# The drain of a fused attention and layer-norm kernel, reordered

## The chip, the cores and the metric

The kernel runs on one core of a Trainium2 chip. The metric is device time in microseconds (us), median of several executions. The profile is one execution of the same program, seen by the hardware profiler; its times count from the first instruction. Engines: PE multiplies matrices (PEld loads its weights), DVE, ACT and POOL work on vectors, SP issues transfers.

## The reference

Inputs: x (4096 x 512), adj (4096 x 4096, about 0.4% of it entries up to 1e9, the diagonal among them), W (512 x 4 heads x 512), a (4 x 1024). All are 32-bit floats.

```
ht  = (x @ W) per head                            # 4 x 4096 x 512
e   = leaky_relu(src[i] + dst[j], 0.01) + adj     # src, dst: ht times the halves of a
att = softmax(e) over j
out = layernorm(x + mean over heads of att @ ht)
```

Where one entry of a row of adj leads all others by far, the softmax is one there and zero elsewhere, in every head. Then row i is layernorm(x[i] + x[j] @ mean of W over heads), with j the column of the row's largest entry. The kernel computes that for all rows, tests with a bound on src and dst whether every row's lead suffices, and has a general path for the case that one doesn't. With these inputs the general path isn't entered.

## The kernel before

There are 32 row blocks of 128 rows. For each block the kernel loads 2 MB of adj (line 127; blocks 28 to 30 in two pieces, block 31 in four), DVE takes maxima of short segments of each row (203), the best segment (210) and its place (212). POOL fetches that segment of the row again by an indirect transfer (223, tile lead); DVE finds the column in it (264) and the second largest value (258, find_inner). For block 31 the column is searched in the whole row at once (272). POOL gathers the x rows of the columns (244, 249; tile y). PE transposes them (278), ACT copies the result (280; tile yt), PE multiplies with the mean of W (297). x itself is added on PE by a matmul with the identity (290, residual).

The schedule is written out by hand: each engine runs its instructions in the order in which the program emits them, across all engines. Loop step t takes adj of block t, the column of block t - 2, the product of block t - 3, the statistics of block t - 4 on ACT (356 to 364) and, a few steps later, the normalisation on ACT (finish, 382). For the statistics' square root comes first root (367), then a reciprocal on DVE and two small instructions on POOL (rstd). Transfers go out on SP in order; a buffer of adj is reused after six blocks, so load t + 5 is issued in step t.

Behind the loop comes the drain. Blocks 24 to 27 (BEHIND to LATE - 1) were put by without x (347), and x is added behind their late load (351, POOL for 24 to 26 and DVE for 27). ACT makes the statistics of 24 to 26 and POOL their factors with a power (375 to 377); for 27 to 31 DVE does it with BN instructions (moments, 402 to 408; factor, 411; normalise, 418). Block 31 is multiplied in two halves (391). The bound of the test needs the square norm of every row of x (row_norm, 341; a maximum over all, 489 to 499); the test (505 to 511) sets a flag for each row, PE counts them (515), DVE makes of that the number of bad rows of each block and in all (519 to 522). Stores go out on SP: 0 to 23 as they become ready, then 28 and 29, 24 and 25, 26 and 27, 30, 31 (666 to 668).

In `tile("px", bufs=1)` one PSUM buffer serves the steps of the bound and the count in turn.

Of the kernel before, what the change touches and what calls it, by code (L numbers as in the profile page):

```python
# [21 lines left out]
P = 128  # L22
C = 512
# [9 lines left out]
@with_exitstack  # L33
def gat_resnorm_kernel(
    ctx: ExitStack,
    tc: tile.TileContext,
    x: bass.AP,
    adj: bass.AP,
    W: bass.AP,
    a: bass.AP,  # L40
    out: bass.AP,
):

    nc = tc.nc
# [12 lines left out]
    leading_rows(tc, x, adj, W, a, out, ident, n_bad, any_bad)  # L65

    flag = nc.values_load(any_bad[0:1, 0:1], min_val=0, max_val=N)
    with tc.If(flag > 0, preferred_fallthrough_block=True, label="general"):
        general(tc, x, adj, W, a, out, ident, n_bad)


@with_exitstack
def leading_rows(ctx, tc, x, adj, W, a, out, ident, n_bad, any_bad):

# [16 lines left out]
    BEHIND = LATE - Q  # L91

    landing = ctx.enter_context(tc.tile_pool(name="landing", bufs=1))
    landing.tile([P, 56], F32, name="pad")
    hold = landing.tile([P, NB, D], F32, name="hold")
    a_rows = landing.tile([2 * H, D], F32, name="a_rows")
    adj_pool = ctx.enter_context(tc.tile_pool(name="adj_pool", bufs=AHEAD + 1))
# [88 lines left out]
    nm = once.tile([P, NB], F32, name="nm")  # L186
    sd = once.tile([P, NB], F32, name="sd")
    lead_by = once.tile([P, 1], F32, name="lead_by")

    def span_of(ib):  # L190
        return next(k for k, (_, lo, hi) in enumerate(spans) if lo <= ib < hi)
# [68 lines left out]
    def find_column(ib):  # L260
        if ib < BEHIND:
            find_inner(ib)
        within = small.tile([P, 8], U32, name="within")
        nc.vector.max_index(within, top[:, ib, :], lead_of[ib])  # L264
# [18 lines left out]
    def turn(ib):  # L283
        yt_of[ib] = turned_rows(y_t.pop(ib))
# [54 lines left out]
    def row_norm(ib):  # L339
        sq = rows.tile([P, D], F32, name="sq")  # L340
        nc.scalar.activation(sq, hold[:, ib, :], AF.Square, accum_out=xx[:, ib : ib + 1])  # L341
# [7 lines left out]
    def add_x(engine, ib):  # L349
        o = o_ps[ib] = o_ps["by"][:, ib - BEHIND, :]  # L350
        engine.tensor_add(o, o, hold[:, ib, :])

    def stats(ib):
        o, i = o_ps[ib], slice(ib, ib + 1)
# [11 lines left out]
    def root(i):  # L366
        nc.scalar.activation(sd[:, i], sd[:, i], AF.Sqrt, bias=eps, scale=1.0 / D)

    def rstd(i):
        nc.vector.reciprocal(sd[:, i], sd[:, i])  # L370
# [114 lines left out]
    def bound(part):  # L485

        if part == 0:
            xm = once.tile([P, 1], F32, name="xm")
            nc.vector.tensor_reduce(xm, xx, axis=AX.X, op=OP.max)
            px = of_bound[0] = psum.tile([1, P], F32, name="px", bufs=1)  # L490
            nc.tensor.transpose(px, xm, ident)
        elif part == 1:
            nc.vector.tensor_reduce(xg, of_bound[0], axis=AX.X, op=OP.max)
        elif part == 2:
            pb = of_bound[2] = psum.tile([P, 1], F32, name="px", bufs=1)
            nc.tensor.matmul(pb, ones[0:1, :], xg, start=True, stop=True)
        else:
            nc.vector.tensor_mul(lead_by, of_bound[2], vn)
            nc.vector.tensor_scalar(lead_by, lead_by, 1.05, 110.0, op0=OP.mult, op1=OP.add)

    gap = once.tile([P, NB], F32, name="gap")

    def test():
        a1 = top[:, :, 0]
        nc.vector.tensor_tensor(gap, top[:, :, 1], inner[:, :, 1], op=OP.max)
        size = once.tile([P, NB], F32, name="size")
        nc.vector.scalar_tensor_tensor(size, a1, -1.0, a1, op0=OP.mult, op1=OP.max)
        nc.vector.tensor_sub(gap, a1, gap)
        nc.vector.tensor_scalar(size, size, -(2.0 ** -22), lead_by, op0=OP.mult, op1=OP.subtract)
        nc.vector.scalar_tensor_tensor(gap, gap, 0.9999, size, op0=OP.mult, op1=OP.add)  # L510
        nc.vector.tensor_scalar(gap, gap, 0.0, None, op0=OP.is_gt)

    def count():
        pg = psum.tile([1, NB], F32, name="px", bufs=1)
        nc.tensor.matmul(pg, ones[:, 0:1], gap, start=True, stop=True)
        return pg

    def report(pg):
        nc.vector.tensor_scalar(n_bad, pg, -1.0, float(P), op0=OP.mult, op1=OP.add)
        total = once.tile([1, 1], F32, name="total")  # L520
        nc.vector.tensor_reduce(total, pg, axis=AX.X, op=OP.add)
        nc.vector.tensor_scalar(any_bad, total, -1.0, float(N), op0=OP.mult, op1=OP.add)

    x_at = {lo - 1 - lo // (5 * Q): (lo, Q) for lo in range(Q, BEHIND, Q)}
    squares = list(range(KB * H))
    squares_at = {t: 2 if t < 7 else 1 for t in range(3, 15)}
    COLUMN, PROJECT, STATS, BEHIND_ROOT = 2, 3, 4, 3
    FACTORS = (*((lo, lo + Q) for lo in range(0, BEHIND - Q, Q)), (BEHIND - 4, BEHIND - 2), (BEHIND - 2, BEHIND))
    FINISHED = {t: (t - 11,) for t in range(11, 28)}
    FINISHED |= {28: (17, 18), 29: (19, 20), 30: (21,), 31: (22,)}  # L530
    WHOLE = range(12, 20)
    END = (*range(1, 3), *range(5, 20))

    for t in range(NB):
# [2 lines left out]
        if t in x_at:  # L537
            load_x(*x_at[t])
        if t + AHEAD == NB - 1:
            load_x(LATE, Q)  # L540
        load_adj(t + AHEAD)
        middle = PIECES if t in END else 1 if t == NB - 1 else 2
        segment_maxima(t, 0, middle)
        if t >= COLUMN and t not in END and t != COLUMN + 1:
            find_column(t - COLUMN)
        if t not in END:
# [7 lines left out]
        if t + 1 in TABLED:  # L554
            clear_rows(t + 1)
        for lo, hi in FACTORS:
            if t == hi - 1 + STATS + BEHIND_ROOT:
                rstd(slice(lo, hi))
        if t < 2:
            mean_of_heads(t)  # L560
        elif t == 2:
# [97 lines left out]
    stats_of_half(NB - 1, 0)  # L659
    factor(NB - 2)  # L660
    normalise(NB - 2, o_ps.pop(NB - 2))
# [7 lines left out]


@with_exitstack
def general(ctx, tc, x, adj, W, a, out, ident, n_bad):

# [173 lines left out]
```

## Time and profile before

| | |
|---|---|
| median of 3 runs (lowest to highest) | 234.12 us (234.05 to 234.87) |
| the profiled execution | 234.12 us, its span 232.6 us |
| PE, DVE, ACT, POOL busy | 193.3, 191.2, 145.2, 105.6 us |
| moved by DMA | 96.32 MB, mean 414 GB/s |
| read from HBM, written to it | 88.54 MB, 8.39 MB |
| last store issued | 228.44 us |

The span runs from the first instruction to the last; the other 1.5 us lie around it. In the profile a line of a group names its source line, engine, operation, out<-in tiles and count, then busy time, mean ns of one, and the idle time of the engine before it with what ended it. A line of a timeline gives start, length, engine, line and tiles; idle time stands in brackets.

### The profile page before, as it was taken

What the parts mean: (1) busy time and instruction counts of PE and PEld (TensorE: products, weight loads), DVE (VectorE), ACT (ScalarE), POOL (GpSimd) and SP (SyncE); (2) the same over time, 40 slices, a digit from 0 to 9 for tenths busy, and PEclk for the clock granted to TensorE, in tenths of its full rate; (3) what the DMA queues carried; (4) which work ended last, traced back from release to release, by engine and by line L of the source; (5) the groups of instructions that cost most, each with busy time, mean ns of one, the idle gap of its engine ahead of it and who ended that gap; (6) DMA issues with size and microseconds to landing.
All of it is one profiled execution on the core that took longest, in us unless ns stands there. A gap on an engine that the chain in (4) does not pass through costs nothing.

```text
span 232.6 us, 2428 instructions
## 1 busy us (share of the span) xinstructions
PE 193.3 (83%) x581; PEld 92.5 (40%) x588; DVE 191.2 (82%) x300; ACT 145.2 (62%) x356; POOL 105.6 (45%) x239
## 2 busy tenths in 40 slices
PE   0068988788099998998999789979999989899990
PEld 0023443343044443443444344445444444445460
DVE  0448289899969997999799959987999999888881
ACT  3004113588076986797998578647777775399661
POOL 4020514515554556355635665644444545548300
PEclk9999999999769999999999999999999999999999
DMA  6999999999999999999999999999999999999985
GB/s 226 430 428 435 424 434 420 438 427 409 440 426 427 418 435 432 437 412 425 443 420 424 426 435 423 418 433 427 428 430 417 425 423 417 420 420 419 426 366 201
DMA packets 12834, 96.32 MB, mean 414 GB/s; under 512 B 2093, under 2 KB 2541, under 8 KB 7056
## 3 DMA queue, kind: packets, MB, share of 16 engines
q1 hardware_dynamic: 9216, 88.08, 89.7%
q0 software_dynamic: 3584, 8.03, 8.8%
q8 instruction: 5, 0.08, 0.1%
q14 instruction: 13, 0.11, 0.1%
q10 hardware_dynamic: 16, 0.02, 0.0%
HBM read 88.54 MB, written 8.39 MB: 417 GB/s over the span
## 4 chain that ended last, share of the span: by engine, by line
DMA 57%; DVE 23%; PE 9%; ACT 4%; issue 3%; POOL 2%; DVEq 0%; POOLq 0%; ACTq 0%
DMA adj_t<-in_adj_dram 54%; DVE seg L203 19%; PE o L297 5%; DMA y<-in_x_dram,col 3%; ACT sq L341 2%; PE o L391 2%; DVE at L212 1%; DVE top L210 1%; PE tp L278 1%; DMA a_rows<-in_L_gnn_a_dram 1%; PE o L290 1%; POOL lead L223 1%; ACT hold L382 1%; DVE within L264 1%; ACT adj_t L347 1%
## 5 line engine op out<-in xcount | busy, mean ns | idle before, releaser
L203 DVE TENSOR_REDUCE seg<-adj_t 128x128 f32<-128x2048 f32 (+5 forms) x58 | 143.8, 2496 | 30.2 <-DMA adj_t<-in_adj_dram 30.1
L297 PE MATMUL o<-w_sum,yt 128*128 128x512 f32 x248 | 113.2, 596 | 2.0 <-ACT yt L280 1.8
L297 PEld LDWEIGHTS o<-w_sum,yt 128*128 128x128 f32 x248 | 45.9, 191 | 52.6 <-issue 41.8
L223 POOL DMA_INDIRECT lead<-in_adj_dram,row x32 | 32.7, 1022 | 14.7 <-POOL row L219 14.7
L219 POOL TENSOR_TENSOR row<-at,first 128x1 uint32<-128x1 uint32 x32 | 6.0, 189 | 65.0 <-DVE at L212 46.3
L280 ACT COPY yt<-tp 128x512 f32<-128x512 f32 x33 | 19.1, 580 | 25.6 <-PE tp L278 25.4
L278 PE MATMUL tp<-ident,y 128*128 128x128 f32 x128 | 22.5, 299 | 12.9 <-DMA y<-in_x_dram,col 12.9
L278 PEld LDWEIGHTS tp<-ident,y 128*128 128x128 f32 x128 | 18.8, 208 | 26.7 <-issue 19.6
L290 PE MATMUL o<-hold,ident 128*128 128x512 f32 x52 | 27.4, 613 | 0.6 <-issue 0.6
L442 PE MATMUL o<-hold,ident 128*128 128x512 f32 x32 | 15.6, 645 | 14.8 <-DMA hold<-in_L_gnn_W_dram 14.8
L249 POOL DMA_INDIRECT y<-in_x_dram,col x20 | 21.6, 1082 | 7.8 <-POOL col L266 5.2
L341 ACT ACTIVATE sq<-hold 128x512 f32<-128x512 f32 x32 | 19.9, 624 | 0.0
L382 ACT ACTIVATE hold<-hold,nm,sd 128x512 f32<-128x512 f32 x24 | 19.0, 803 | 0.0
L327 ACT ACTIVATE off<-px,minus 128x128 f32<-128x128 f32 x20 | 7.3, 367 | 17.7 <-PE px L325 17.6
L364 ACT ACTIVATE sq<-hold,nm 128x512 f32<-128x512 f32 x24 | 17.3, 722 | 0.8
L443 ACT ACTIVATE w_sum<-o 128x512 f32<-128x512 f32 x4 | 2.4, 597 | 22.6 <-PE o L442 22.6
L337 PE MATMUL o<-z,pick 128*128 128x512 bf16 x54 | 15.4, 389 | 0.6 <-ACT off L327 0.4
L442 PEld LDWEIGHTS o<-hold,ident 128*128 128x128 f32 x32 | 6.5, 208 | 23.2 <-issue 21.2
L362 ACT ACTIVATE hold<-o 128x512 f32<-128x512 f32 x24 | 14.3, 597 | 0.8
L244 POOL DMA_INDIRECT y<-in_x_dram,col x12 | 11.9, 996 | 5.5 <-POOL col L266 5.2
L210 DVE MAX8 top<-seg 128x8 f32<-128x256 f32 (+2 forms) x32 | 11.6, 362 | 1.1
L239 ACT COPY y<-zero 128x512 f32<-128x512 f32 x20 | 12.1, 603 | 0.0
(116 smaller groups left out, 177.3 us busy)
## 6 DMA issues: line engine op xcount, KB each, us to landing
adj_t<-in_adj_dram SPq DMA_DIRECT2D x28, 2048.0 KB
hold<-in_x_dram SPq DMA_DIRECT2D x6, 1024.0 KB
adj_t<-in_adj_dram SPq DMA_DIRECT2D x6, 1024.0 KB
hold<-in_L_gnn_W_dram SPq DMA_DIRECT2D x2, 2048.0 KB
out_dram<-hold SPq DMA_DIRECT2D x7, 512.0 KB
out_dram<-hold SPq DMA_DIRECT2D x3, 1024.0 KB
adj_t<-in_adj_dram SPq DMA_DIRECT2D x4, 512.0 KB
hold<-in_x_dram SPq DMA_DIRECT2D x2, 512.0 KB
```

The source lines that it names most:

```text
L203: nc.vector.tensor_reduce(seg_of[ib][:, ts(k, N // e // n)], adj_t[ib][:, ts(k, N // n)].rearrange("p (s e) -> p s e", e=e), axis=AX.X, op ...
L223: nc.gpsimd.indirect_dma_start(out=lead, out_offset=None, in_=adj_segs[e], in_offset=bass.IndirectOffsetOnAxis(ap=row[:, :1], axis=0),)
L249: nc.gpsimd.indirect_dma_start(out=y_t[ib], out_offset=None, in_=x, in_offset=bass.IndirectOffsetOnAxis(ap=col[:, :1], axis=0), bounds_che ...
L278: nc.tensor.transpose(tp[:, kb, :], y[:, ds(kb, P, KB)], ident)
L280: nc.scalar.copy(yt, tp)
L290: nc.tensor.matmul(o_ps[ib], ident, hold[:, ib, :], start=start, stop=False)
L297: nc.tensor.matmul(o_ps[ib], yt_of[ib][:, kb, :], w_sum[:, kb, :], start=(start and kb == 0), stop=(kb == KB - 1),)
L337: nc.tensor.matmul(o_ps[ib], pick, z[k], start=(start and k == 0), stop=False)
L341: nc.scalar.activation(sq, hold[:, ib, :], AF.Square, accum_out=xx[:, ib : ib + 1])
L364: nc.scalar.activation(sq, hold[:, ib, :], AF.Square, bias=nm[:, i], scale=-float(D), accum_out=sd[:, i])
L382: nc.scalar.activation(hold[:, ib, :], o, AF.Identity, bias=nm[:, i], scale=sd[:, i])
L442: nc.tensor.matmul(o, ident, hold[:, w_at + kb * H + h, :], start=(h == 0), stop=(h == H - 1))
```

## The change

The drain and the steps that lead into it are reordered, and some of their work is done in another way:

- x of 28 to 31 was one load ahead of adj of 31. Now x of 28 and 29 stays there, and x of 30 and 31 goes behind adj of 31, between that of 24 and 25 and that of 26 and 27.
- Block 28 gets its x by DVE, PSUM plus x into PSUM, instead of a matmul; 29's residual matmul moves one step later.
- The factors of blocks 20 to 23 are made one step earlier, those of 22 and 23 on POOL a step behind their reciprocal. finish of 21 and 22 moves ahead in step 30, that of 23 into step 31.
- Row norms of 28 and 29 stay in step 31; 30 and 31 join the late ones.
- On POOL the adds of x to 24 and 25 go behind the gather of 30, the gather of 31's rows goes ahead of the fetch of its segment, and the adds to 26 and 27 follow; DVE adds no x to 27 any more.
- The factors of 24 and 25 and those of 26 are made apart.
- The test has five instructions instead of six, its last one also sums the flags of a row (accum_out), and it stands behind the normalisation of 29. The bound is one ACT instruction. The count is a 128x1 matmul ahead of the halves of 31, and the report one instruction; the counts for each block are made in the general path.

```diff
+    leads = keep.tile([P, NB], F32, name="leads")
...
-    landing.tile([P, 56], F32, name="pad")
+    landing.tile([P, 24], F32, name="pad")
...
+    def add_sums(ib, out):
+        nc.vector.tensor_add(out, o_ps[ib], hold[:, ib, :])
+        o_ps[ib] = out
...
-            nc.vector.tensor_mul(lead_by, of_bound[2], vn)
-            nc.vector.tensor_scalar(lead_by, lead_by, 1.05, 110.0, op0=OP.mult, op1=OP.add)
+            nc.scalar.activation(lead_by, of_bound[2], AF.Identity, bias=floor, scale=vn)
...
-        nc.vector.tensor_scalar(size, size, -(2.0 ** -22), lead_by, op0=OP.mult, op1=OP.subtract)
-        nc.vector.scalar_tensor_tensor(gap, gap, 0.9999, size, op0=OP.mult, op1=OP.add)
-        nc.vector.tensor_scalar(gap, gap, 0.0, None, op0=OP.is_gt)
+        nc.vector.scalar_tensor_tensor(
+            size, size, 2.0 ** -22, lead_by.to_broadcast([P, NB]), op0=OP.mult, op1=OP.add
+        )
+        nc.vector.scalar_tensor_tensor(
+            leads, leads, 0.9999, size, op0=OP.mult, op1=OP.is_gt, accum_out=leading
+        )
...
     def report(pg):
-        nc.vector.tensor_scalar(n_bad, pg, -1.0, float(P), op0=OP.mult, op1=OP.add)
-        total = once.tile([1, 1], F32, name="total")
-        nc.vector.tensor_reduce(total, pg, axis=AX.X, op=OP.add)
-        nc.vector.tensor_scalar(any_bad, total, -1.0, float(N), op0=OP.mult, op1=OP.add)
+        nc.vector.tensor_scalar(any_bad, pg, -1.0, float(N), op0=OP.mult, op1=OP.add)
...
-            load_x(LATE, Q)
+            load_x(LATE, 2)
...
-            for ib in (BEHIND, BEHIND + 2):
+            for ib in (BEHIND, LATE + 2, BEHIND + 2):
                 load_x(ib, 2)
...
+        if t == NB - 2:
+            finish(BEHIND - 3)
+            finish(BEHIND - 2)
         if t == NB - 1:
-            for late in range(LATE, NB):
-                row_norm(late)
-        if t == NB - 2:
-            residual(LATE)
+            row_norm(LATE)
+            row_norm(LATE + 1)
+            finish(BEHIND - 1)
             residual(LATE + 1)
...
-    finish(BEHIND - 1)
-    for ib in range(BEHIND, LATE):
+    for ib in (BEHIND, LATE + 2, BEHIND + 2):
         row_norm(ib)
-    nc.scalar.activation(xx, xx, AF.Sqrt)
+        row_norm(ib + 1)
+    nc.scalar.activation(xx, xx, AF.Sqrt, scale=1.05 ** 2)
...
-    add_x(nc.gpsimd, BEHIND)
     find_column(NB - 2)
+    add_x(BEHIND)
+    add_x(BEHIND + 1)
+    find_column_in_row(NB - 1)
     fetch_segment(NB - 1)
-    add_x(nc.gpsimd, BEHIND + 1)
-    find_column_in_row(NB - 1)
-    add_x(nc.gpsimd, BEHIND + 2)
+    add_x(BEHIND + 2)
+    add_x(BEHIND + 3)
...
+    add_sums(LATE, o_ps[LATE])
     moments(LATE)
...
+    late_factors(slice(BEHIND, BEHIND + 2))
     factor(LATE)
     normalise(LATE, o_ps.pop(LATE))
-    for ib in range(BEHIND, NB):
+    bound(3)
+    for ib in range(BEHIND, NB - 1):
         find_inner(ib)
-    bound(3)
-    test()
     turn(NB - 2)
     stats(BEHIND + 2)
-    late_factors(slice(BEHIND, BEHIND + 3))
+    late_factors(slice(BEHIND + 2, BEHIND + 3))
     products(NB - 3, KB - 1, KB)
-    pg = count()
     products(NB - 2, 0, KB - 1)
-    report(pg)
+    finish(BEHIND)
     moments(NB - 3)
     factor(NB - 3)
     normalise(NB - 3, o_ps.pop(NB - 3))
+    find_inner(NB - 1)
+    test()
+    finish(BEHIND + 1)
     turn(NB - 1)
     products(NB - 2, KB - 1, KB)
-    add_x(nc.vector, LATE - 1)
-    finish(BEHIND)
-    finish(BEHIND + 1)
+    pg = count()
     moments(LATE - 1)
     finish(BEHIND + 2)
     products_of_half(NB - 1, 0)
     products_of_half(NB - 1, 1)
-    nc.vector.tensor_add(hold[:, NB - 2, :], o_ps[NB - 2], hold[:, NB - 2, :])
-    o_ps[NB - 2] = hold[:, NB - 2, :]
-    moments(NB - 2)
+    add_sums(NB - 2, hold[:, NB - 2, :])
+    report(pg)
     factor(LATE - 1, shift=True)
     finish(LATE - 1)
+    moments(NB - 2)
     stats_of_half(NB - 1, 0)
...
+        column = alone.tile([P, 1], F32, name="column")
+        nc.vector.memset(column, 1.0)
...
+        ps = pps.tile([2 * H, C], F32, name="ps_sd")
+        nc.tensor.matmul(ps[:1, :NB], column, leads, start=True, stop=True)
+        nc.vector.tensor_scalar(n_bad, ps[:1, :NB], -1.0, float(P), op0=OP.mult, op1=OP.add)
```

More of the change, by code (lines that the diff above doesn't have):

```diff
@@ L63, in gat_resnorm_kernel, with leading_rows @@
     any_bad = keep.tile([1, 1], I32, name="any_bad")
-    leading_rows(tc, x, adj, W, a, out, ident, n_bad, any_bad)
+    leads = keep.tile([P, NB], F32, name="leads")
+    leading_rows(tc, x, adj, W, a, out, ident, leads, any_bad)
     flag = nc.values_load(any_bad[0:1, 0:1], min_val=0, max_val=N)
     with tc.If(flag > 0, preferred_fallthrough_block=True, label="general"):
-        general(tc, x, adj, W, a, out, ident, n_bad)
+        general(tc, x, adj, W, a, out, ident, leads, n_bad)
 @with_exitstack
-def leading_rows(ctx, tc, x, adj, W, a, out, ident, n_bad, any_bad):
+def leading_rows(ctx, tc, x, adj, W, a, out, ident, leads, any_bad):
     nc = tc.nc
@@ L188, in leading_rows @@
     lead_by = once.tile([P, 1], F32, name="lead_by")
+    floor = once.tile([P, 1], F32, name="floor")
+    nc.gpsimd.memset(floor, 110.0)
     def span_of(ib):
@@ L347, in put_by, with add_x @@
         nc.scalar.copy(o_ps["by"][:, ib - BEHIND, :], o_ps.pop(ib))
-    def add_x(engine, ib):
+    def add_x(ib):
         o = o_ps[ib] = o_ps["by"][:, ib - BEHIND, :]
-        engine.tensor_add(o, o, hold[:, ib, :])
+        nc.gpsimd.tensor_add(o, o, hold[:, ib, :])
+    def add_sums(ib, out):
+        nc.vector.tensor_add(out, o_ps[ib], hold[:, ib, :])
+        o_ps[ib] = out
     def stats(ib):
@@ L367, in root, with scales @@
         nc.scalar.activation(sd[:, i], sd[:, i], AF.Sqrt, bias=eps, scale=1.0 / D)
-    def rstd(i):
-        nc.vector.reciprocal(sd[:, i], sd[:, i])
+    def scales(i):
         nc.gpsimd.tensor_mul(nm[:, i], nm[:, i], sd[:, i])
@@ L497, in bound @@
         else:
[L498 to L501 removed]
+            nc.scalar.activation(lead_by, of_bound[2], AF.Identity, bias=floor, scale=vn)
+    leading = once.tile([P, 1], F32, name="leading")
     def test():
         a1 = top[:, :, 0]
[L505 removed]
+        nc.vector.tensor_tensor(leads, top[:, :, 1], inner[:, :, 1], op=OP.max)
         size = once.tile([P, NB], F32, name="size")
         nc.vector.scalar_tensor_tensor(size, a1, -1.0, a1, op0=OP.mult, op1=OP.max)
[L508 to L511 removed]
+        nc.vector.tensor_sub(leads, a1, leads)
+        nc.vector.scalar_tensor_tensor(
[4 more added lines that the diff above has]
+        )
     def count():
[L514 to L515 removed]
+        pg = psum.tile([1, 1], F32, name="px", bufs=1)
+        nc.tensor.matmul(pg, ones[:, 0:1], leading, start=True, stop=True)
         return pg
     def report(pg):
[L519 to L522 removed]
+        nc.vector.tensor_scalar(any_bad, pg, -1.0, float(N), op0=OP.mult, op1=OP.add)
     x_at = {lo - 1 - lo // (5 * Q): (lo, Q) for lo in range(Q, BEHIND, Q)}
@@ L526, in leading_rows, with lag_of @@
     squares_at = {t: 2 if t < 7 else 1 for t in range(3, 15)}
-    COLUMN, PROJECT, STATS, BEHIND_ROOT = 2, 3, 4, 3
+    COLUMN, PROJECT, STATS = 2, 3, 4
     FACTORS = (*((lo, lo + Q) for lo in range(0, BEHIND - Q, Q)), (BEHIND - 4, BEHIND - 2), (BEHIND - 2, BEHIND))
     FINISHED = {t: (t - 11,) for t in range(11, 28)}
-    FINISHED |= {28: (17, 18), 29: (19, 20), 30: (21,), 31: (22,)}
+    FINISHED |= {28: (17, 18), 29: (19, 20)}
+    def lag_of(hi):
+        return hi - 1 + STATS + (3 if hi < BEHIND - 2 else 2)
     WHOLE = range(12, 20)
@@ L545, in leading_rows @@
             find_column(t - COLUMN)
+            if t == lag_of(BEHIND) + 1:
+                scales(slice(BEHIND - 2, BEHIND))
         if t not in END:
@@ L556, in leading_rows @@
         for lo, hi in FACTORS:
-            if t == hi - 1 + STATS + BEHIND_ROOT:
-                rstd(slice(lo, hi))
+            if t == lag_of(hi):
+                nc.vector.reciprocal(sd[:, lo:hi], sd[:, lo:hi])
+                if hi < BEHIND:
+                    scales(slice(lo, hi))
         if t < 2:
@@ L671, in general @@
 @with_exitstack
-def general(ctx, tc, x, adj, W, a, out, ident, n_bad):
+def general(ctx, tc, x, adj, W, a, out, ident, leads, n_bad):
     nc = tc.nc
```

## The prediction

> **What bounds the kernel now.** I read the page's slices first, then the busy time by stretch, then the chain of waits, then the timeline of each engine and the groups from 200 us on. The transfers' busy share in forty slices of the span:
>
> ```profile
> DMA  6999999999999999999999999999999999999985
> ```
>
> No slice between the first and the last two has a digit under 9. Busy time by stretch (PE, PEld, DVE, ACT, POOL, then granted clock, DMA share, GB/s) says how full that is, and when it ends:
>
> ```profile
> 200.00:205.00 5.00, 4.35 (x13) 2.02 (x13) 4.25 (x9) 1.22 (x3) 2.87 (x8) 1.00 1.02 416
> 215.00:222.00 7.00, 7.00 (x25) 3.44 (x24) 6.00 (x27) 4.06 (x13) 2.43 (x4) 1.00 1.04 427
> 222.00:224.00 2.00, 2.00 (x8) 1.23 (x8) 1.90 (x5) 1.98 (x4) 0.00 (x0) 1.00 0.96 399
> 224.00:226.00 2.00, 2.00 (x12) 1.74 (x10) 1.76 (x7) 1.80 (x5) 0.00 (x0) 1.00 0.85 336
> 226.00:228.00 2.00, 0.38 (x2) 0.00 (x0) 1.15 (x5) 0.45 (x2) 0.00 (x0) 1.00 0.89 359
> 228.00:229.00 1.00, 0.00 (x0) 0.00 (x0) 0.27 (x1) 0.41 (x1) 0.00 (x0) 1.00 0.73 285
> 229.00:230.00 1.00, 0.00 (x0) 0.00 (x0) 0.00 (x0) 0.00 (x0) 0.00 (x0) 1.00 0.77 299
> 230.00:231.00 1.00, 0.00 (x0) 0.00 (x0) 0.00 (x0) 0.00 (x0) 0.00 (x0) 1.00 0.18 70
> ```
>
> SP's timeline shows the stores that feed this:
>
> ```profile
> 209.23 1.62 SPq L437 DMA_DIRECT2D out_dram<-hold  x2
> 221.45 0.33 SPq L437 DMA_DIRECT2D out_dram<-hold  x1
> ...
> 228.44 0.33 SPq L437 DMA_DIRECT2D out_dram<-hold  x1
> ```
>
> SP issues nothing from 210.9 to 221.45, and still the sixteen DMA engines are all busy until 222: they work off stores (up to row block 23) that were ready long before. So the transfer queues and no compute engine bound the kernel up to 222 us. Even the tail is nearly theirs: from 222 to 231 the idle share sums to 0.08 + 0.30 + 0.22 + 0.27 + 0.23 + 0.82 = 1.92 us of the sixteen, the most that a drain without any gap could give back. The share of 0.18 in the last microsecond is three of sixteen engines: a few are behind the rest and end the transfers alone. When the last store (block 31, 256 KB) is issued at 228.44, older ones are still moving: 285 + 299 + 70 GB/s over a microsecond each is 654 KB after 228, so some 400 KB, 0.9 us at 427 GB/s, lies ahead of it, uneven over the engines.
>
> The chain of waits tells another story, because it follows the compute:
>
> ```profile
> 213.20 0.48 ACT yt L280
> ...
> 222.84 3.55 PE o L391 x16
> ```
>
> From block 29's turned rows PE works without a hole to the halves of block 31, which end at 226.39; two microseconds of statistics and factors bring the last store.
>
> **The change, part by part.** Every byte loaded and stored stays. So the terms below move the last compute, and then the question is how much of that the queues let through.
>
> *Loads.* From the groups of DVE in the drain (from 200 us) and the timeline:
>
> ```profile
> L203 DVE TENSOR_REDUCE seg<-adj_t 128x16 f32<-128x1024 f32 (+1 forms) x5 | 7.1, 1426 | 1.0 <-DMA adj_t<-in_adj_dram 1.0
> L272 DVE FIND_INDEX8 col<-top,adj_t 128x8 uint32<-128x4096 f32 x1 | 4.4, 4419 | 0.0
> L418 DVE TENSOR_SCALAR hold<-o,mv,sd 128x512 f32<-128x512 f32 (+1 forms) x3 | 2.2, 719 | 0.1
> ```
>
> ```profile
> 202.57 0.96 POOL L223 DMA_INDIRECT lead<-in_adj_dram,row  x1 [0.51 <-POOL row L219]
> ...
> 208.45 0.07 DVE L264 MATCH_VALUE_LOAD within<-top,lead 128x8 f32 x1
> ```
>
> ```profile
> lead<-in_adj_dram,row POOLq DMA_INDIRECT x32, 5.9
> ```
>
> x of 30 and 31 (512 KB) goes behind adj of 31: its pieces land 512 KB / 0.42 = 1.25 us earlier, and DVE's 1.0 us of waiting in L203 goes. What is late next is block 30's segment. Its gather goes at 202.57, before and after, and by the row of the transfers it takes 5.9 us in the median to land, so until 208.5: exactly where L264 starts now. DVE then waits there instead, and the search in 31's row (L272, 4.42 us) starts at 208.7 as before. I count 0 for this part (bounds 0 and -1.0, if the gather is quicker).
>
> *PE's start.*
>
> ```profile
> 201.02 1.98 PE L290 MATMUL o<-hold,ident 128*128 128x512 f32 x4 [0.65 <-issue]
> ```
>
> ```profile
> L341 ACT ACTIVATE sq<-hold 128x512 f32<-128x512 f32 x8 | 4.9, 620 | 0.0
> ```
>
> The residual matmuls of 28 and 29 (1.98 us behind a wait for x) leave the place before block 27; 29's half of them, 1.0 us, comes back one block later. ACT has two row norms (0.62 us each) instead of four ahead of 28's turned rows, but six instead of four ahead of 29's, and the x of 26 and 27 that the last two need still comes last in the load queue. I take 0.6 us for 29's turned rows, between 0 and 1.2, half of two norms: PE starts there at about 213.1 instead of 213.7. The count's matmuls leave this stretch too, 0.2 us. So block 31 could be turned by 220.6.
>
> *Rows of 31 and the POOL queue.* POOL's timeline, and the transposes of 31 on PE:
>
> ```profile
> 210.84 0.21 POOL L219 TENSOR_TENSOR row<-at,first 128x1 uint32<-128x1 uint32 x1
> 211.32 0.96 POOL L223 DMA_INDIRECT lead<-in_adj_dram,row  x1 [0.27 <-POOL row L219]
> 212.29 1.29 POOL L351 TENSOR_TENSOR adj_t<-adj_t,hold 128x512 f32<-128x512 f32 x1
> 213.88 0.96 POOL L244 DMA_INDIRECT y<-in_x_dram,col  x1 [0.30 <-PE o L387]
> 214.86 1.28 POOL L351 TENSOR_TENSOR adj_t<-adj_t,hold 128x512 f32<-128x512 f32 x1
> 219.84 0.19 POOL L375 TENSOR_SCALAR sd<-sd 128x3 f32<-128x3 f32 x1 [3.70 <-ACT sq L358]
> 220.11 0.90 POOL L376 TENSOR_TENSOR sd<-sd,power 128x3 f32<-128x3 f32 x1
> 221.09 0.20 POOL L377 TENSOR_TENSOR nm<-nm,sd 128x3 f32<-128x3 f32 x1
> ```
>
> ```profile
> 221.35 0.63 PE L278 MATMUL tp<-ident,y 128*128 128x128 f32 x4
> ```
>
> The search ends at 213.1, and the add that ran until 213.58 is over by then, since the segment's fetch no longer stands before it: 31's gather goes at 213.5 instead of 213.88. At today's distance, at most 221.35 - 213.88 = 7.5 us, the rows are there by 221.0, and PE is free at 220.6. The halves could start at about 222.1 instead of the 222.84 of the chain, 0.6 to 0.7 us earlier.
>
> POOL takes that back. Behind 31's gather, from 214.4, now stand the fetch (0.21, a gap of 0.27, 0.96), two adds (2 x 1.28) and only then the factors of 24 and 25 (219.84 to 221.29, 1.45 us for three columns; two could be cheaper, I keep it): 215.9, 218.4, 219.9. On ACT the finish of 24 waits for them, and the root for 29 is now queued behind that finish, with 25's finish and 31's turned rows:
>
> ```profile
> 223.92 0.28 ACT L408 ACTIVATE sd<-mv,eps 128x1 f32<-128x1 f32 x1
> 224.11 0.80 ACT L382 ACTIVATE hold<-adj_t,nm,sd 128x512 f32<-128x512 f32 x1
> ```
>
> So finish runs 219.9 to 220.7, the root ends at 221.0, the reciprocal and 29's normalisation (0.7 to 0.8; L418's mean has one of half width in it) at 222.0. That is 0.6 us later than the 221.45 at which its store goes now.
>
> *The test* stands behind that normalisation, and PE has the count ahead of 31's halves:
>
> ```profile
> 217.41 0.20 DVE L505 TENSOR_TENSOR gap<-top,inner 128x32 f32<-128x32 f32 x1
> ...
> 218.28 0.18 DVE L511 TENSOR_SCALAR gap<-gap 128x32 f32<-128x32 f32 x1
> ```
>
> Six instructions took 218.46 - 217.41 = 1.05 us; five and the find_inner of 31 take about the same, 222.0 to 223.1. DVE's accumulated output isn't in this trace; it costs between -0.2 and +0.2, a small instruction either way, and I take 0. The count needs another 0.2: the halves start at about 223.4 instead of 222.84, and PE, the tail and the last store (229.0) are **0.6 us later**. The rest (three instructions of report become one, the bound goes from two on DVE to one on ACT, 28's sum made by DVE in PSUM, the count in the general path that isn't entered) lies beside PE's products and ahead of nothing late: 0, and 0.7 us each, a DVE pass, if that cover is gone.
>
> *Through the queues.* The store of 31 is issued 0.6 us later into queues that had 0.9 us of older work before it, most of it on the few late engines that end alone; the stores of 24 to 27 and 30 keep those fed. I let +0.1 of it through (bounds 0 and +0.6); of a gain of 0.7 the late engines would let at most 0.3 through. The profiled execution took 234.12 us, its span of 232.6 and 1.5 around it, and is the median of the runs: **234.2 us**, no change that can be told, where 0.5% (1.17 us) is about what a measurement of this kernel tells from none.
>
> One rule speaks against splitting the load of 28 to 31 in two. The Trainium skill, "DMA: Bandwidth & Descriptors", section "Anatomy of one DMA — SWDGE (gpsimd) path", fits about 2.0 us fixed plus bytes over 436 GB/s to each transfer, so the extra one would cost 2 us, an estimate by that page. The trace speaks against it: share 1.02 at 200 to 205 us, where pieces of 512 KB move.
>
> **The rivals.**
> *A, the forecast*: compute 0.6 us later, hidden by the queues. For it: share 1.04 until 222 with nothing issued for 10 us. 234.2, chance 0.55.
> *B, the drain gets shorter*: 29's root isn't held, the halves start at 222.1. With the 0.3 that the late engines allow, 233.8; with no gap at all in the tail, 1.92 less, 232.2. Against it is the order on ACT and POOL. Chance 0.26, 0.12 of it under 232.95, since I read the late engines from mean shares alone.
> *C, slower by the count*: 31's segment, now fetched behind its rows, decides. Issued at 214.9 plus 5.9 it lands at 220.8, before find_inner wants it at 222.0. If it takes the 7.5 us that 31's rows may take, and 0.6 more behind them, it lands at 223.0, the halves start at 224.4, 1.6 late; the queues are empty by then and pass on about 1.2: 235.3. It decides from a landing after 222.0. Chance 0.15.
> *D, transfers that don't overlap*: the extra transfer exposes its latency. The last store, with little behind it, needs from 228.44 to about 231, 2.5 us, of which 0.6 are its bytes; 1.9 exposed gives 236.0. Against it is the full share where small pieces move. Chance 0.04. The skill's fit would come to the same time.
>
> **How the numbers follow.** The likeliest is A, 234.2. The range, 233.0 to 235.3, holds A with its bounds (234.1 to 234.7), B down to the middle between 233.8 and 232.2, and C's price. Faster by over 0.5% (under 232.95): 0.12, B with hardly a gap left. Slower by over 0.5% (over 235.29): half of C, 0.08, and D, 0.04. The same: 0.76.
>
> **What would show it.** Right: DMA shares of 1.0 until 222 and about 0.9 behind; the last store issued at about 229; L264 of 30 waiting for its gather; ACT idle before the finish of 24 until about 219.9; PE idle about 1 us before the count. Wrong: the halves starting before 222.2 (B), or a hole of over 2 us on PE before the count with DVE waiting for 31's segment (C); a DMA share under 0.95 between 200 and 215 (D). The argument fails as a whole if the last transfer ends over 1 us earlier although the bytes are the same.

## The result, and the profile after

The changed kernel takes 235.86 us (median of 6 runs, 235.46 to 236.20) against 234.18 us before (6 runs, 234.05 to 234.87): a ratio of 1.0066, interval 1.0051 to 1.0081, or 1.7 us more. The forecast was 234.2 us and no change that can be told; the time lies above its range.

The page of the changed kernel, its span and the transfers' share in forty slices:

```profile
span 234.2 us, 2438 instructions
...
DMA  6999999999999999999999999999999999999982
```

This execution took 235.88 us; its span is 1.6 us longer than the 232.6 before. The slices say little: the last two digits changed from 85 to 82, in slices that are themselves longer. Busy time by stretch of the changed kernel, columns as in the prediction:

```profile
215.00:222.00 7.00, 7.00 (x25) 3.42 (x24) 3.67 (x15) 6.00 (x16) 5.66 (x10) 1.00 1.04 428
222.00:224.00 2.00, 1.50 (x7) 0.61 (x6) 1.90 (x10) 0.59 (x2) 0.00 (x0) 1.00 0.89 371
...
228.00:229.00 1.00, 0.00 (x0) 0.00 (x0) 0.69 (x3) 0.57 (x2) 0.00 (x0) 1.00 0.76 279
229.00:230.00 1.00, 0.00 (x0) 0.00 (x0) 0.09 (x1) 0.23 (x1) 0.00 (x0) 1.00 0.25 98
230.00:231.00 1.00, 0.00 (x0) 0.00 (x0) 0.00 (x0) 0.00 (x0) 0.00 (x0) 1.00 0.73 270
231.00:232.00 1.00, 0.00 (x0) 0.00 (x0) 0.00 (x0) 0.00 (x0) 0.00 (x0) 0.95 0.10 35
```

The queues are full until 222 as before. At the end there is a hole: the share falls to 0.25 in 229 to 230, and the last store then fills 230 to 231 almost alone. The kernel before has a shorter hole that whole microseconds hide: taken by quarters, its share is 0.27 and 0.28 from 228.75 to 229.25, and 0.88 in the quarter behind. In both kernels the bytes of the last store begin to move about 0.8 us behind its issue.

The timeline of the changed kernel (start, length, engine, line), cut to the steps that the prediction gives times for:

```profile
208.52 0.09 DVE L267 MATCH_VALUE_LOAD within<-top,lead 128x8 f32 x1 [1.09 <-DMA lead<-in_adj_dram,row]
213.28 0.57 ACT L283 COPY yt<-tp 128x512 f32<-128x512 f32 x1
213.97 0.95 POOL L247 DMA_INDIRECT y<-in_x_dram,col  x1 [0.85 <-PE o L393]
220.30 0.81 ACT L388 ACTIVATE hold<-adj_t,nm,sd 128x512 f32<-128x512 f32 x1 [0.37 <-POOL nm L383]
221.02 0.28 ACT L414 ACTIVATE sd<-mv,eps 128x1 f32<-128x1 f32 x1
221.53 0.81 DVE L424 TENSOR_SCALAR hold<-o,mv,sd 128x512 f32<-128x512 f32 x1
222.51 0.22 DVE L510 TENSOR_TENSOR leads<-top,inner 128x32 f32<-128x32 f32 x1
223.23 0.08 DVE L517 DVE_READ_ACCUMULATOR leads<-leads,size 128x1 f32 x1
223.49 3.72 PE L397 MATMUL o<-w_sum,yt 128*128 128x256 f32 x16
224.64 0.14 DVE L527 TENSOR_SCALAR any_bad<-px 1x1 int32<-1x1 f32 x1
...
229.26 0.33 SPq L443 DMA_DIRECT2D out_dram<-hold  x1
```

L388 is finish of 24, L414 the root for 29, L424 its normalisation, L510 the start of the test and L397 the halves of 31. These are close to the forecast. What the forecast passed over is L527, the flag that decides whether the general path is entered. It is written at 224.78; before, it was there at 219.23:

```profile
219.09 0.14 DVE L522 TENSOR_SCALAR any_bad<-total 1x1 int32<-1x1 f32 x1
```

Who reads that flag, and what follows, stands in the views of the source lines of the sequencers: count, shortest, median and longest in ns, first and last start. Of the kernel before:

```profile
L67 POOLq TENSOR_LOAD <-any_bad x1: 504/504/504, 221.1 to 221.1; - x1
L68 POOLq INC_SWDGE_SEM  x1: 1476/1476/1476, 222.6 to 222.6; - x1
L844 POOLq EVENT_SEMAPHORE  x4: 17/17/17, 231.8 to 232.5; - x4
L844 POOLq DRAIN  x3: 40/103/5306, 224.1 to 232.3; - x3
L844 SPq DRAIN  x3: 7/7/7, 231.7 to 232.0; - x3
```

Of the changed kernel:

```profile
L68 POOLq TENSOR_LOAD <-any_bad x1: 773/773/773, 224.8 to 224.8; - x1
L69 POOLq INC_SWDGE_SEM  x1: 1476/1476/1476, 226.6 to 226.6; - x1
L866 POOLq EVENT_SEMAPHORE  x4: 17/17/17, 233.4 to 234.1; - x4
L866 POOLq DRAIN  x3: 40/103/5306, 228.1 to 234.0; - x3
L866 SPq DRAIN  x3: 7/7/7, 232.6 to 233.7; - x3
```

POOL's sequencer loads the flag, branches, spends 1.48 us on INC_SWDGE_SEM and 5.31 us in a DRAIN. SP's first DRAIN stands behind its semaphores for the stores. Before, POOL's long DRAIN ended at 224.1 + 5.3 = 229.4; POOL then stood until 231.8, just behind SP's 231.7. After, it ends at 228.1 + 5.3 = 233.4, exactly where POOL's next semaphore starts, and SP had been ready since 232.6. None of this counts as busy, and the chain of waits doesn't show it: there both kernels seem to end with the halves of 31 and its normalisation.

So two chains race to the end: the last store with SP's closing, and the flag with POOL's. Both got later, and POOL's now decides.

### The profile page after: what moved, and what is told of

Same layout as the page of the kernel before. It is cut to its first block, busy times and chain, and to the rows that moved or that the text cites. A ratio compares the mean times of both kernels' runs of the same rounds, so it can differ in the third digit from the quotient of the medians.

```text
span 234.2 us, 2438 instructions
## 1 busy us (share of the span) xinstructions
PE 193.5 (83%) x586; PEld 92.3 (39%) x586; DVE 190.4 (81%) x296; ACT 145.7 (62%) x357; POOL 107.6 (46%) x244
## 4 chain that ended last, share of the span: by engine, by line
DMA 57%; DVE 29%; POOL 6%; issue 4%; PE 2%; ACT 1%; DVEq 0%; POOLq 0%; ACTq 0%
DMA adj_t<-in_adj_dram 53%; DVE seg L206 22%; DMA lead<-in_adj_dram,row 3%; DVE at L215 2%; POOL lead L226 2%; POOL adj_t L354 2%; PE o L397 2%; DVE top L213 1%; DVE col L275 1%; DVE within L267 1%; DMA a_rows<-in_L_gnn_a_dram 1%; POOL y L247 1%; POOL row L222 0%; ACT hold L388 0%; DVE hold L424 0%
## 5 line engine op out<-in xcount | busy, mean ns | idle before, releaser
L448 PE MATMUL o<-hold,ident 128*128 128x512 f32 x32 | 15.9, 653 | 14.5 <-DMA hold<-in_L_gnn_W_dram 14.5
L293 PE MATMUL o<-hold,ident 128*128 128x512 f32 x50 | 26.5, 612 | 0.0
L388 ACT ACTIVATE hold<-hold,nm,sd 128x512 f32<-128x512 f32 x24 | 18.9, 801 | 0.7 <-POOL sd L378 0.7
L340 PE MATMUL o<-z,pick 128*128 128x512 bf16 x60 | 16.9, 392 | 0.3 <-ACT pick L332 0.3
```

Source lines behind the costliest of these rows:

```text
L293: nc.tensor.matmul(o_ps[ib], ident, hold[:, ib, :], start=start, stop=False)
L340: nc.tensor.matmul(o_ps[ib], pick, z[k], start=(start and k == 0), stop=False)
L388: nc.scalar.activation(hold[:, ib, :], o, AF.Identity, bias=nm[:, i], scale=sd[:, i])
L448: nc.tensor.matmul(o, ident, hold[:, w_at + kb * H + h, :], start=(h == 0), stop=(h == H - 1))
```

## The experiments

All times are compared with the kernel before on the same chip. This table gathers them (us; the end of POOL's long DRAIN is its start plus 5.3; "later" is the difference of the medians):

| kernel | flag | last store | POOL's DRAIN ends | SP's first DRAIN | span | median | later |
|---|---|---|---|---|---|---|---|
| before | 219.2 | 228.44 | 229.4 | 231.7 | 232.6 | 234.18 | |
| after | 224.8 | 229.26 | 233.4 | 232.6 | 234.2 | 235.86 | 1.68 |
| e1 after, report early | 224.0 | 229.25 | 232.9 | 231.8 | 233.7 | 235.33 | 1.10 |
| e2 after, count last | 227.2 | 228.73 | 235.7 | 232.6 | 236.6 | 237.99 | 3.76 |
| e3 before, flag late | 226.4 | 228.61 | 235.0 | 232.4 | 235.8 | 237.40 | 3.17 |
| e4 before, store late | 219.2 | 229.35 | 229.4 | 233.0 | 233.9 | 235.40 | 1.17 |
| e5 after, test back | 220.9 | 230.43 | 230.3 | 233.8 | 234.6 | 235.76 | 1.54 |
| e6 e5 and root first | 219.9 | 229.37 | 229.3 | 232.6 | 233.5 | 235.20 | 0.98 |
| e7 after, root first | 223.5 | 227.96 | 231.8 | 232.0 | 232.9 | 235.03 | 0.81 |
| e8 before, loads split | 219.9 | 229.06 | 230.0 | 231.8 | 232.6 | 234.31 | 0.09 |
| e9 e6 and bound first | 219.7 | 229.21 | 229.4 | 232.6 | 233.5 | 235.18 | 0.79 |
| e10 e7 and e1 | 223.3 | 228.56 | 231.6 | 232.2 | 233.1 | 234.90 | 0.51 |
| e11 e10, segment first | 223.2 | 228.78 | 232.2 | 232.5 | 233.4 | 235.13 | 0.74 |
| e12 after, POOL busy | 225.6 | 230.04 | 233.9 | 233.2 | 234.8 | 236.40 | 2.00 |

In all fourteen rows the span ends 0.8 to 0.9 us behind the later of the two columns on the DRAINs. That is the finding; the runs below were made to reach it one at a time.

**e1, the report earlier.** The flag is computed as soon as the count is there, ahead of the last step of moments(27).

```diff
-    def moments(ib):
+    def moments(ib, pg=None):
...
+        if pg is not None:
+            report(pg)
         mv = mean_var[ib] = small.tile([P, nc.vector.BN_AGGR_DIM], F32, name="mv", bufs=3)
...
-    moments(LATE - 1)
+    moments(LATE - 1, pg)
...
-    report(pg)
```

> The changed kernel with one move: the report of the flag stands on DVE between the two statistics instructions of block 27 instead of behind them and 30's sum. Theory 1 (POOL's closing steps follow the flag: from the flag to the end of the span the changed kernel shows 9.4 us, and that chain ends last): the flag comes 0.7 us earlier (224.06 instead of 224.78), the last store is not touched, the stores' own end takes over at 233.4 of the span, and the time falls by 0.7 us to 235.1. Theory 2 (the late last store alone makes the changed kernel slower): 235.8 to 235.9, no change against it.

Measured: 235.33 us, ratio 1.0043 (1.0027 to 1.0059). The flag came 0.8 earlier, the last store was issued at 229.25 as in the changed kernel, and the time fell by 0.5 instead of 0.7: POOL's load of the flag took 1.10 us here and 0.77 there. The two intervals overlap, but five of the six runs lie below every run of the changed kernel. Its closing lines:

```profile
L867 POOLq EVENT_SEMAPHORE  x4: 17/17/17, 232.9 to 233.6; - x4
L867 POOLq DRAIN  x3: 40/103/5306, 227.6 to 233.5; - x3
L867 SPq DRAIN  x3: 7/7/7, 231.8 to 233.2; - x3
```

POOL still decides: its next semaphore at 232.9 stands at the end of its DRAIN (227.6 + 5.3). SP's closing moved too, from 232.6 to 231.8, although the last store was issued at the same time; the part on e8 comes back to that. It isn't the later of the two in either kernel, so the 0.5 is the flag's.

**e2, the count last.** The count goes behind the halves of 31 and the report behind their statistics, so the last store should be early and the flag late: the two theories now point in opposite directions.

```diff
     products(NB - 2, KB - 1, KB)
-    pg = count()
...
     products_of_half(NB - 1, 1)
+    pg = count()
     add_sums(NB - 2, hold[:, NB - 2, :])
-    report(pg)
...
     stats_of_half(NB - 1, 1)
+    report(pg)
```

> The changed kernel with PE's count behind the two halves of block 31 and the report behind the last statistics instruction of DVE. The halves then start about 1 us earlier, the last store is issued at 229.1 to 229.2 (DVE's queue holds it), the flag comes at about 227.5. Theory 1: the end is the flag plus 9.4 us, a time of 238.5 (+2.7 against the changed kernel). Theory 2: 235.7 to 235.9.

Measured: 237.99 us, 1.0157 (1.0140 to 1.0173). The last store is issued 0.5 earlier than in the changed kernel, and yet the kernel is 2.1 us slower than that one. The flag came 0.3 earlier than expected, at 227.2, and the time is 0.5 under the 238.5 of theory 1.

```profile
L866 POOLq DRAIN  x3: 40/103/5306, 230.4 to 236.3; - x3
L866 SPq DRAIN  x3: 7/7/7, 232.6 to 236.0; - x3
```

**e3, only the flag late in the kernel before.**

```diff
     products(NB - 2, 0, KB - 1)
-    report(pg)
     moments(NB - 3)
...
     normalise(NB - 2, o_ps.pop(NB - 2))
+    report(pg)
     stats_of_half(NB - 1, 1)
```

> The kernel before with one move: the three instructions of the report stand on DVE ahead of the statistics of the second half of 31, in idle time of that engine, so that the last store isn't moved. The flag comes at about 226.3 instead of 219.2. Theory 1: span 226.3 + 9.4 = 235.7, time 237.3 (+3.1 against before). Theory 2: 234.2, no change.

Measured: 237.40 us, 1.0134 (1.0117 to 1.0150): 3.2 us for moving three tiny instructions.

```profile
226.27 0.14 DVE L522 TENSOR_SCALAR any_bad<-total 1x1 int32<-1x1 f32 x1
...
L844 POOLq DRAIN  x3: 40/103/5306, 229.7 to 235.5; - x3
L844 SPq DRAIN  x3: 7/7/7, 232.4 to 235.2; - x3
```

The last store was issued at 228.61, 0.17 later than before. In after, e1, e2, e3 and e12, where POOL ends last, the span ends 9.2 to 9.8 us behind the flag. This shows the first cause.

**e4, only the last store late in the kernel before.** The statistics of 31's second half are made three times, to the same values.

```diff
     stats_of_half(NB - 1, 1)
+    stats_of_half(NB - 1, 1)
+    stats_of_half(NB - 1, 1)
     moments(NB - 1)
```

> The kernel before with the statistics of the second half of 31 made three times instead of once: the last store is issued about 0.8 us later, the flag and every other store stay. If the queues absorb a late last store, as the prediction had it: 234.2 to 234.4. If they pass it on: 235.0.

Measured: 235.40 us, 1.0047 (1.0033 to 1.0061). The store is issued 0.91 later, the time is 1.17 longer, and SP's closing goes from 231.7 to:

```profile
L846 POOLq DRAIN  x3: 40/103/5306, 224.1 to 233.6; - x3
L846 SPq DRAIN  x3: 7/7/7, 233.0 to 233.3; - x3
```

The flag and POOL's long DRAIN are where they were. So the stores' end alone can make the kernel slower: here SP's closing is 1.3 later, more than the store. The next run shows that a late store need not pass.

**e8, the loads alone in the kernel before.** Load of x split in two, norms of 30 and 31 with the late ones.

```diff
-            load_x(LATE, Q)
+            load_x(LATE, 2)
...
-            for ib in (BEHIND, BEHIND + 2):
+            for ib in (BEHIND, LATE + 2, BEHIND + 2):
                 load_x(ib, 2)
...
-            for late in range(LATE, NB):
+            for late in range(LATE, LATE + 2):
                 row_norm(late)
...
-    for ib in range(BEHIND, LATE):
+    for ib in (BEHIND, LATE + 2, BEHIND + 2):
         row_norm(ib)
+        row_norm(ib + 1)
```

> The kernel before with the new order of loads alone: x of 28 and 29 ahead of adj of 31, x of 30 and 31 behind it, and the row norms of 30 and 31 among the late ones, since they would wait otherwise. The prediction's step: DVE's 1.0 us of waiting for adj turns into a wait for 30's segment, so 234.2, no change. If the extra transfer cost its fixed time: 235 to 236.

Measured: 234.31 us, 1.0006 (0.9995 to 1.0016), no difference. In its profile the last store is issued 0.62 late and SP's closing is only 0.1 late, unlike in e4. How much of a late store passes thus differs between runs: from issue to SP's first DRAIN it is 3.3 us before and after, 2.6 in e1, 2.7 in e8, and up to 4.0 in e7.

The single packets in the traces show where the difference lies. The last store moves as sixteen shares side by side, each closed by a packet of 4 bytes, and SP's first DRAIN stands 0.7 to 0.9 us behind the last share (1.3 in e3). In the changed kernel thirteen shares end by 230.91. The last one starts at 231.08, just as a packet of 8 KB ends (230.50 to 231.08), and lasts until 231.90. That packet is of the queue that the page of the changed kernel calls `instruction` (packets, MB, share):

```profile
q14 instruction: 13, 0.11, 0.1%
```

In e1, whose last store is issued at the same time, two such packets move only from 230.96, and the last share ends at 230.97. The transfers' share in the last microsecond of both, the changed kernel first:

```profile
231.00:232.00 1.00, 0.00 (x0) 0.00 (x0) 0.00 (x0) 0.00 (x0) 0.00 (x0) 0.95 0.10 35
231.00:232.00 1.00, 0.00 (x0) 0.00 (x0) 0.00 (x0) 0.00 (x0) 0.00 (x0) 1.00 0.00 0
```

Two such packets move near the end of all fourteen profiles. In before, e1, e3 and e8 the first starts when at most three shares are left, and the last share ends 0.1 to 0.7 us behind the fourth from last; in the other ten it starts earlier, and the last share trails by 0.8 to 1.4. So a last store 0.6 to 0.8 us later than before moved SP's closing by 0.1 where these packets came behind it (e1, e8), and a store 0.8 to 0.9 later moved it by 0.9 to 1.3 where they came ahead (after, e4). No run was made to move the packets alone, and what decides when they come isn't shown.

**e5, e6, e9: the test back in its old place**, ahead of the turn of 30, with the segment of 31 fetched ahead of the adds so that it can be there. e6 adds "moments(NB - 3)" ahead of "finish(BEHIND)", which takes the root of 29 out from behind POOL's factors; e9 adds the bound ahead of the statistics of 25 on ACT. The core of e9:

```diff
+    fetch_segment(NB - 1)
     add_x(BEHIND)
-    add_x(BEHIND + 1)
     find_column_in_row(NB - 1)
-    fetch_segment(NB - 1)
+    add_x(BEHIND + 1)
...
     bound(2)
+    bound(3)
     stats(BEHIND + 1)
...
-    for ib in range(BEHIND, NB - 1):
+    for ib in range(BEHIND, NB):
         find_inner(ib)
+    test()
...
     products(NB - 3, KB - 1, KB)
+    pg = count()
     products(NB - 2, 0, KB - 1)
-    finish(BEHIND)
+    report(pg)
     moments(NB - 3)
+    finish(BEHIND)
```

> The changed kernel with the test, the count and the report back at their places of before (behind block 28's normalisation, the count ahead of the first products of 30), for which 31's segment is fetched ahead of its rows again. Everything else of the change stays. The flag should come at about 219.2 and the halves of 31 start at 222.6, as before. Theory 1 with the late store (both costs come from the place of the test): all of the loss goes, 234.2 (234.0 to 234.4), the same as before. If another part of the change costs (the split load, the sums in PSUM, the POOL order): between 234.6 and 235.9.

> The same with one more move: ACT makes the root for block 29 ahead of the finish of 24. ACT then turns 31 a little earlier, the halves start at about 222.3 and the last store goes at about 228.1, 0.3 us earlier than before. If the queues pass that on: 233.9, faster than before by 0.3. If the late engines end it: 234.1.

> The test back at its early place and the root for 29 first, with one more move: ACT makes the bound ahead of the statistics of 25. In the run before this the bound stood behind them on ACT, they waited 1.1 us for POOL's add, and the test, the count and PE waited with them (1.6 us of PE). If that new wait was what kept the time at 235.2: the flag at 219, the halves at 222.2 to 222.6, the last store at 228.0 to 228.4, a time of 233.9 to 234.3, the same as before. If a part of the change that is still in it costs: 234.8 or more.

Measured: 235.76 (1.0060, 1.0043 to 1.0076), 235.20 (1.0042, 1.0028 to 1.0056) and 235.18 us (1.0040, 1.0024 to 1.0055). None comes to the time of before, which would have shown the test's place as the only cost; e5 and e9 lie where another part of the change was expected to cost, e6 outside what was expected. The flag is early again (219.7 to 220.9) and POOL's closing no longer decides, but the last store is 0.8 to 2.0 late. The timeline of e9 shows where:

```profile
214.72 3.71 POOL L354 TENSOR_TENSOR adj_t<-adj_t,hold 128x512 f32<-128x512 f32 x3
216.91 1.60 DVE L510 TENSOR_TENSOR leads<-top,inner 128x32 f32<-128x32 f32 x1
218.44 0.20 DVE L512 SCALAR_TENSOR_TENSOR size<-top 128x32 f32<-128x32 f32 x1
219.32 0.19 PE L523 MATMUL px<-leading,ones 128*1 128x1 f32 x2 [1.48 <-ACT sq L363]
```

L510, 0.22 us in the changed kernel, takes 1.60 here and ends at 218.51, right behind the three adds of POOL (218.43). In e5 it took 1.42 and ended at 219.74, with POOL's adds at 219.66. PE has the count ahead of its products, so it stands for 1.48 us, and the tail comes later with it. (The view blames ACT's L363, which was done long before.) The reason that I took for e5, the bound queued on ACT behind 25's statistics, fell with e9, where the bound is early and PE stands as long.

**e12, adds beside the test.** Two more adds on POOL in the changed kernel, into a part of a buffer that nobody reads.

```diff
     late_factors(slice(BEHIND + 2, BEHIND + 3))
+    for _ in range(2):
+        nc.gpsimd.tensor_add(o_ps["by"][:, 4, :], hold[:, 0, :], hold[:, 0, :])
```

> The changed kernel with two more adds on POOL behind the factors of 26, into a part of a buffer that nobody reads: POOL is busy from 221.5 to about 224.0 and so while DVE begins the test at 222.5. In the two runs with the early test its first instruction (two operands in SBUF) took 1.4 and 1.6 us instead of 0.2 and ended with POOL's adds. If POOL's adds hold up such an instruction of DVE: the test ends about 1.5 us later, the flag comes at about 226.2, PE's halves start at 225.0, and the time is 237.3. If those two had another cause: 235.9, since the additional adds come ahead of nothing on POOL but its reading of the flag.

Measured: 236.40 us, 1.0076 (1.0053 to 1.0100). From its timeline:

```profile
221.34 2.23 POOL L656 TENSOR_TENSOR adj_t<-hold 128x512 f32<-128x512 f32 x2
...
222.44 0.21 DVE L510 TENSOR_TENSOR leads<-top,inner 128x32 f32<-128x32 f32 x1
222.57 1.06 DVE L512 SCALAR_TENSOR_TENSOR size<-top 128x32 f32<-128x32 f32 x1
```

L512, 0.21 us without the adds, takes 1.06 and ends at 223.63, POOL's adds at 223.57. The halves start 0.78 later, as do the flag and the last store. The time is 0.5 over that of the changed kernel, about a third of what was expected, since the adds were over sooner than I had counted; the two intervals overlap, so the trace carries the argument here and not the time. L512 ends with POOL's second add, as L510 ended with the last add in e5, e6 and e9: POOL's adds hold up DVE's test. The Trainium skill, "SBUF — State Buffer", section "SBUF: two separate sides", calls the port pair that DVE and GpSimd share an exclusive lock, held for a whole instruction, against DVE operations with two inputs in SBUF. These lengths agree, and so does L510 in e12, which took its usual 0.21: POOL's first add had ended at 222.38 and the second began at 222.46, so L510 began at 222.44 between them. In e9 each add began 0.04 to 0.05 us before the one ahead of it ended, and L510, begun beside the second, was held until the third was done.

**e7, e10, e11: can the changed kernel be mended?** e7 moves one line; e10 is e7 with e1; e11 is e10 with the fetch of 31's segment ahead of the adds and the early bound of e9.

```diff
-    finish(BEHIND)
     moments(NB - 3)
+    finish(BEHIND)
     factor(NB - 3)
```

> The changed kernel with that move alone: the root for block 29 ahead of the finish of 24, so that the normalisation of 29 no longer waits for POOL's factors (2.1 us of idle time on DVE). The test then waits for 31's segment, which lands at 221.5 to 221.9 by the completion records, instead of 222.26. So the flag, the halves and the last store come 0.4 to 0.7 us earlier: 235.3. If the late factors of 24 were the whole reason for the late test: 234.9 or less.

> The changed kernel with the root for 29 ahead of the finish of 24 and the report between the statistics instructions of 27: two moves, the test stays behind 29's normalisation. Theory 1: the flag comes 0.7 us earlier than with the root alone (235.03) until the stores' end takes over: 234.4 to 234.6. Theory 2 (the last store alone): 235.0, since the store goes as with the root alone.

> The kernel of the last line with the segment of 31 fetched ahead of its rows again, an add of x between them, and the bound ahead of 25's statistics on ACT. The late test then waits neither for POOL's factors nor for the segment (1.0 us of idle time on DVE): flag at about 221.5, halves at 222.0 to 222.3, last store at 227.8 to 228.1. If flag and last store are all that the change costs: 233.9 to 234.2, the changed order with its late test is as fast as before.

Measured: 235.03 (1.0036, 1.0024 to 1.0047), 234.90 (1.0024, 1.0014 to 1.0034) and 235.13 us (1.0035, 1.0022 to 1.0047). e7 gains 0.8, a little more than expected. e10 is the best of the changed kernels, and still measurably slower than the one before; it missed the 234.4 to 234.6 of theory 1 and lies near the 235.0 of theory 2. In both POOL's closing is already ahead of SP's (231.8 and 232.0 in e7, 231.6 and 232.2 in e10), so an earlier flag had nothing left to give. e11 missed its 233.9 to 234.2 by 0.9. What is late in e10, from its timeline:

```profile
221.55 0.23 DVE L261 MAX8 inner<-lead 128x8 f32<-128x64 f32 x1 [1.23 <-DMA lead<-in_adj_dram,row]
```

With the root out of the way, the test waits for the segment of 31, which is fetched behind its rows: rival C's mechanism, 1.2 us of it (1.0 in e7). e11 fetches it first and that wait is gone, but then the add to 25 comes later on POOL, ACT's statistics of 25 wait for it, PE stands 0.83 us for the turned rows of 30, and nothing is won. No kernel here is faster than the one before.

## Why the prediction was wrong

*The queues bound until 222 us*: right, the share is 1.04 there.

*Loads, 0*: right. L267 of 30 waits 1.09 us for its gather, as foretold, and e8 measures ratio 1.0006. The 2 us that the Trainium skill's fit ("DMA: Bandwidth & Descriptors", "Anatomy of one DMA — SWDGE (gpsimd) path") would have put on the split are not there: e8 is 0.09 us from the kernel before. That section is about transfers that GpSimd issues, and these loads go out on SP.

*PE starts at 213.1 rather than 213.7*: wrong by 0.8, without effect. 29's turned rows are copied at 213.28 to 213.85, behind six row norms; there was no gain, and 0.2 of loss, just outside my bounds. 31's gather went at 213.97 rather than 213.5.

*The price on POOL*: right. Finish of 24 at 220.30 (forecast 219.9), the root until 221.30 (221.0), normalisation until 222.34 (222.0).

*The test and the count, 0.6 late*: right. The halves start at 223.49 (223.4). The accumulated output cost one small instruction of 0.08 us, inside -0.2 to +0.2. The last store was issued 0.82 late instead of 0.6; the rest came behind the halves' start.

*The rest, with "three instructions of report become one", lying "ahead of nothing late: 0"*: **this step failed.** I followed the report by its cost on DVE and not by who reads its result. I had the flag's move in hand (the test 5 us later in the same text) and didn't follow it to POOL's closing, because the page counts no sequencer instruction as busy and the chain of waits ends elsewhere. POOL's DRAIN ended 2.3 us ahead of SP's closing before; the flag moved by 5.6, of which 1.9 were covered since POOL read the old flag only at 221.1, behind its factors. e2 and e3 show it: in e3 a flag moved alone costs 3.2 us.

*"I let +0.1 of it through"*: **mis-sized too**, and would have been enough for a wrong answer. SP's closing went from 231.7 to 232.6, by all of the 0.8 that the store was late. The 654 KB behind the "some 400 KB, 0.9 us at 427 GB/s" were counted from 228, while the store is issued at 228.44. At the 402 GB/s of these quarters, about 180 KB had moved by then, which leaves about 220 KB, or 0.5 us, and much of that on three late engines. The late engines themselves were read rightly: before, three shares of the last store end at 230.56, 230.69 and 230.78, all others by 230.30, and in e1 and e8 stores 0.81 and 0.62 late move SP's closing by 0.1. What the prediction didn't have is the packets of the instruction queue, which stand ahead of two shares of the last store in the changed kernel. That they make the difference is read from the packets' times; no run moved them alone.

The two don't add. The span ends 0.8 us behind the later of SP's 232.6 and POOL's 233.4. With an early flag it would end behind SP: at 233.5, as in e6 and e9, or at about 232.7 if those packets came late as in e1. POOL's closing so adds 0.7 to 1.5 of the 1.6.

*The rivals.* B (halves at 222.1) didn't come; e7's profile has them at 222.18 once the root of 29 isn't held, and its store at 227.96, which supports the working of B, yet that run's SP closing is no earlier than before. C gave a time near the one measured, 235.3, but by luck and not by its mechanism, which shows only in e7 and e10. D is excluded by e8.

Open: what sets the time at which the two packets of the instruction queue come, and so whether they stand ahead of the last store. In e10, whose last store is issued 0.12 later than before and whose SP closes 0.5 later, fourteen shares end by 230.19 and the last two at 231.44 and 231.45, with those packets from 230.14 to 230.56 ahead.

## What to carry to other kernels

Before moving the result that decides a branch, follow it to every engine that reads it and add what that engine does behind the branch until the program ends: sequencer instructions count as nothing in busy time and can still end last. The mean backlog of the transfer queues isn't the slack of the last transfer: look at it in fractions of a microsecond, and test it by making only that transfer late, in more than one way. A small DVE operation on two operands in SBUF isn't to be put beside POOL's adds when PE waits for it.

## What had not been expected of the hardware

POOL's end took 1.48 us of INC_SWDGE_SEM and 5.31 us of DRAIN in all fourteen profiles, so that the span ended 9.2 to 9.8 us behind the flag in every kernel in which POOL ended last. A 128x32 DVE operation of 0.2 us took 1.06, 1.42, 1.60 and 1.62 us (e12, e5, e9, e6) beside POOL's 128x512 adds, ending 0.06 to 0.09 us behind them. Two 8 KB packets of the instruction queue near the end of the program stood ahead of shares of the last store in ten of fourteen profiles, and its last share then ended 0.8 to 1.4 us behind the fourth from last.
